# A two-layer graph network on one core: attributes' linear scores made in layer 0, codes loaded two steps ahead, a narrower placing product

## The chip, the cores and the metric

The kernel runs on one core of a Trainium2 chip. The core has a TensorE (PE, with its weight loads shown apart as PEld), a VectorE (DVE), a ScalarE (ACT), a GpSimd (POOL) and a SyncE (SP), and 16 DMA engines. The metric is the device time in microseconds of one execution; the median of three runs stands for a kernel. Three runs of the kernel before took 3234.09, 3242.03 and 3247.2 us.

## The reference, cut to what matters

There are N = 3125 nodes with 128 features, and E = 100,000 edges sorted by destination; each edge has a source, a destination, 16 attributes and one of 4 relations.

```python
# layer 0
mean = segment_sum(x[src], dst) / max(deg, 1)
h = layernorm(x + elu(mean @ W0 + b0))
# layer 1: an attention over each (node, relation)
xl = einsum('nf,rfh->nrh', h, W_l) + b_l          # 4 heads of 128: 512 columns
xr = einsum('nf,rfh->nrh', h, W_r) + b_r
z  = xl[src, type] + xr[dst, type] + edge_attr @ W_e[type, :16] + rel_emb[type] @ W_e[type, 16:]
score[e, h] = sum_c leaky_relu(z)[e, h, c] * att[type, h, c]
alpha = softmax of score over the edges of one (dst, type)
h_msg = weighted mean over relations and heads of segment_sum(alpha * xl[src, type])
# then layernorm, a feed-forward block, layernorm, and an outer residual layernorm
```

`leaky_relu(z) = 0.8 relu(z) + 0.2 z`. So a score has a part with relu, and a part that is linear in z: 0.2 times a sum over channels of z times att. The linear part of the edge's attributes is a product of the 16 attributes with a small vector for each head and relation ("v2" below). The linear part of xl is kept in four more columns of the table of xl.

## The kernel before, in words

Edges are taken in tiles of 128; 784 tiles (TT) make 196 quads of four tiles (NQ, index u) and 98 groups of eight tiles (NGR). The work is in three parts: a prologue, layer 0, and layer 1 with a short tail.

**Order.** In both layers a wrapper class `Ordered` (L637) ties each engine's instructions to the order in which the Python code issues them, so each engine runs a list written by hand; the profile therefore shows nearly all of them under one line, L647. SP issues the loads and stores, POOL the gathers.

**Prologue (L767 to L925).** It turns sources, destinations and types into layouts by edge, and writes two tables to DRAM: `seg_d` (for each edge a code of relation and place in its window) and `rm_d` (masks for the segmented scans). It makes `tm`, a bf16 tile of 128 x 3136 which says for each edge which of the four relations is its own (L859).

**Layer 0 (L927 to L1352).** A loop over steps s, one quad per step from quad 52 on (the first 52 quads are handled by counting). In a step PE sums gathered rows of x by destination (`sums0`), ACT copies the sums (`out_copy`), PE places them (`out0`), DVE adds them (`add0`). Other work hangs on given steps through `at_step`: weights in steps 3 to 11, counting in steps 3 to 41, and for each of 25 blocks of 128 nodes a chain that ends in a burst of products (`tables`, `half`) which write 512 columns of xl and xr for four relations to DRAM. Attributes come in with edges on partitions; `turned` (L1112) transposes them for four quads at once into `emt`, and `keep` stores that to the DRAM table `eat_d`, in 49 such groups spread over the steps by `turned_at` (L1087). `edge_weights` (L980) makes the vectors of the scores: `attw` for the part with relu and `vw` for the linear part. In step NS, `rows_of_sources` turns `tm` in place into a mask of 0 and -1e30 (`tng`).

**Layer 1 (L1355 to L1719).** A loop over steps s with software pipelining: `part(f, s, lag, every, n)` calls f for the quad or group that is `lag` steps behind. For a quad u:

- `load_rows` one step ahead: on SP, in this order, `er` (attributes, 256 KB, repeated for four relations, 2 buffers), `sg` (codes, 128 KB, repeated on all partitions, 3 buffers), for even u four loads of `rm` (32.1 KB each), then one, two or four windows of xr, `win` (14 buffers; one for u under 80, two under 152, four after that). `load` has POOL gather four tiles of rows of xl, 258 KB each.
- `distance` (ACT: `far` from `sg`), `onehots` (DVE: `oht` from `sg`), `masked` (DVE: `ea` from `far` and `er`).
- one step later for each of four heads: `z_of` (PE: eight or more products into one bank of PSUM) and `relu` (ACT), then `score` (PE: four products of 32 columns of weights into `row`). `score_edges` (L1497) opens the bank `row` with four products `vw` x `ea`.
- `linear` (DVE: `lx` from the mask `tng` and the four extra columns of xl), which `score_end` adds to `row` by a transpose.
- then the segmented softmax per group, and eight steps later (`LATE`) `sums`, `sums_out`, `spread` (DVE: `ohq`, a one-hot of 128 x 128), `add_sums_p` (PE: `fo`, 128 columns) and `add_sums` (DVE adds 64 of those columns to `acc1`).

Of the kernel before, what the change touches and what calls it, by code (L numbers as in the profile page):

```python
# [9 lines left out]
F32 = mybir.dt.float32  # L10
I32 = mybir.dt.int32
U16 = mybir.dt.uint16
BF16 = mybir.dt.bfloat16
AF = mybir.ActivationFunctionType
OP = mybir.AluOpType
# [5 lines left out]
P = 128  # L21
# [3 lines left out]
R = 4  # L25
H = 4
HC = H * F
# [13 lines left out]
BIG = 1.0e30  # L41
# [3 lines left out]
F32R = mybir.dt.float32r  # L45
# [645 lines left out]
def windows(ctx: ExitStack, tc: tile.TileContext, a, out, flag):  # L691
# [5 lines left out]
    rm_d = S["rm_d"] = dram.tile([TT, RW], BF16, name="rm_d")  # L697
    fl_d = dram.tile([3, TT], F32, name="fl_d")
    eat_d = dram.tile([NQ, 2 * DE, 512], F32, name="eat_d")
    xl_d = dram.tile([NP * R, XW], F32, name="xl_d")  # L700
    xr_d = dram.tile([NP * R * 2, HC], F32, name="xr_d")
    h_d = dram.tile([NB2, P, F], F32, name="fh_d")
# [9 lines left out]
    pid = cst.tile([P, 1], I32, name="pid")  # L712
    ir = cst.tile([P, R], F32, name="ir")
    attw = cst.tile([P, H, 2, WA], F32, name="attw")
    vw = cst.tile([P, 2, WA], F32, name="vw")
    tm = tng = cst.tile([P, TT, R], BF16, name="tmr")
    rv = cst.tile([P, NQ], F32, name="rv")
    weh = cst.tile([P, HC], F32R, name="weh")
    wel = cst.tile([P, HC], F32R, name="wel")
# [31 lines left out]

    with tc.tile_pool(name="l0c", bufs=1) as l0c:
        acc0 = l0c.tile([P, 2, NPW], F32, name="acc0")

        XG, TD = 24, 4 * UD
        xg = l0c.tile([P, XG, F + 1], F32, name="xg")
# [10 lines left out]
        with tc.tile_pool(name="pr", bufs=1) as pr, tc.tile_pool(name="prp", bufs=2, space=PSUM) as prp:  # L767
# [64 lines left out]
            for k, t1 in ((2, 4 * UP), (4, 4 * UQ)):  # L832
# [23 lines left out]
            nc.vector.tensor_scalar_min(dc_i, rF4[:, :UD, 0], float(ND - 1))  # L856
            typ = floats("typ", typi)
            to_e(typ_e, typ)
            nc.vector.tensor_tensor(tm, typ_e.unsqueeze(2).to_broadcast([P, TT, R]),  # L859
                                    ir.unsqueeze(1).to_broadcast([P, TT, R]), op=OP.is_equal)  # L860


            seg = pr.tile([TR, TC, P], BF16, name="seg")
# [63 lines left out]
        with tc.tile_pool(name="m0c", bufs=1) as m0c, tc.tile_pool(name="l0", bufs=2) as l0, \  # L927
# [7 lines left out]
            def at_step(s, eng, f):  # L935
                jobs.setdefault((s, eng), []).append(f)
# [24 lines left out]
            cr = l0e.tile([DR + 1, R], F32, name="cr")  # L961
            nc.vector.memset(cr, 1.0)

            def load_edge_weights():
                for i in range(2):
                    for r in range(R):
                        p0 = r * 2 * DE + i * DE
                        sp.dma_start(we[p0:p0 + DE], a["L1_gnn_W_e"][r, 0:DE, :])
                        sp.dma_start(attr[p0:p0 + DE], bcast(a["L1_gnn_att"][r], HC, DE))
                sp.dma_start(arow, a["L1_gnn_att"].rearrange("r h c -> (r h) c"))  # L970
# [9 lines left out]
            def edge_weights():  # L980
                act.activation(weh, we, AF.Copy)
                ve.tensor_sub(wel, we, weh.bitcast(F32))
                ve.tensor_mul(attr, attr, we)
                v2 = l0e.tile([P, H], F32, name="v2")
                ve.tensor_reduce(v2, attr.rearrange("p (h c) -> p h c", h=H), AX.X, OP.add)
                ve.tensor_scalar(v2, v2, SLOPE, None, op0=OP.mult)
                atp_ = bank()[:, 0, :R * H]
                pe.transpose(atp_, arow, ident[:R * H, :R * H])
                ve.memset(attw, 0.0)
                ve.memset(vw, 0.0)  # L990
                for i in range(2):
                    ve.tensor_copy(vw[:, i, 16 * i:16 * i + 16].rearrange("p (h r) -> p h r", r=R),
                                   v2.unsqueeze(2).to_broadcast([P, H, R]))
                    for h in range(H):
                        ve.tensor_scalar(attw[:, h, i, 16 * i + 4 * h:16 * i + 4 * h + 4],
                                         atp_.rearrange("p (r h) -> p h r", r=R)[:, h], 1.0 - SLOPE, None, op0=OP.mult)

            def places():

                fbv = fb.rearrange("p (u i) -> p u i", i=4)  # L1000
                i4 = l0e.tile([P, 4], F32, name="i4")
                ve.tensor_scalar(i4, iw[:, :4], p5, None, op0=OP.is_equal)
                ve.tensor_scalar(rv, fbv[:, :, 0], -1.0, p31, op0=OP.mult, op1=OP.add)
                for i in range(4):
                    ve.scalar_tensor_tensor(rv, fbv[:, :, i], i4[:, i:i + 1], rv, op0=OP.mult, op1=OP.add)

            def rows_of_sources():

                ve.tensor_scalar(tng, tm, 1.0, BIG, op0=OP.subtract, op1=OP.mult)
                ve.tensor_scalar_min(typ_e, typ_e, float(R - 1))  # L1010
                ve.scalar_tensor_tensor(src_e, src_e, R, typ_e, op0=OP.mult, op1=OP.add)

# [36 lines left out]
            for i, f in enumerate([edge_weights] +  # L1049
                                  [linear_weights(r) for r in range(R)] +  # L1050
                                  [constant(r) for r in range(R)]):
                at_step(3 + i, "ve", f)


            ees, erows = {}, {}
# [29 lines left out]
            NS = NQ - UD  # L1085

            def turned_at(f):  # L1087
                return f * (NS - 6) // (NQ // 4)

            def step_of(u):  # L1090
                return turned_at(u // 4)
# [20 lines left out]
            def turned(us):  # L1112
                mp = bank()
                for j, u in enumerate(us):
                    c, i0 = u // QC, u * 4 % TR
                    pe.transpose(mp[:, j], ees[c][:, i0:i0 + 4].rearrange("p t s d -> p (t s d)"), ident)
                em = l0.tile([P, 4, P], F32R, name="emt", bufs=3)
                act.activation(em, mp, AF.Copy)
                X["emt", us[0]] = em

            def keep(us):
                em = X.pop(("emt", us[0])).bitcast(F32)
                for j, u in enumerate(us):
                    sp.dma_start(eat_d[u].rearrange("x (t e) -> t x e", t=4), em[:, j])
# [189 lines left out]
            for s in range(last + 1):  # L1314
# [18 lines left out]
                    f()  # L1333
                if UD < u <= NQ:
                    out0(u - 1)
                counts = jobs.pop((s, "count"), [])
                for i, v in enumerate(counts):
                    count(v)
# [2 lines left out]
                    count_add(v)  # L1341
                if UD < u <= NQ and not counts:
                    add0(u - 1)
                for e in ("act", "ve"):
                    for f in jobs.pop((s, e), []):
                        f()
# [10 lines left out]
    with tc.tile_pool(name="ac", bufs=1) as ac, tc.tile_pool(name="at", bufs=2) as at, \  # L1357
# [51 lines left out]
        dc = at.tile([16, 1], F32, name="dc", bufs=3)  # L1409
        nc.vector.memset(dc, 0.0)  # L1410
        carry = {"m": mc, "d": dc}
        Q, G = {}, {}
        pe, ve, act, pool, sp = (Ordered(tc, e) for e in (nc.tensor, nc.vector, nc.scalar, nc.gpsimd, nc.sync))
        es = [slice(i * P, (i + 1) * P) for i in range(4)]
        cg = [slice(i * WA, (i + 1) * WA) for i in range(4)]
        hs = [slice(h * F, (h + 1) * F) for h in range(H)]

        def load_rows(u):
            d = Q[u] = {}
            d["er"] = at.tile([P, 512], F32, name="er", bufs=2)  # L1420
            ev = eat_d[u]
            sp.dma_start(d["er"], bass.AP(tensor=ev.tensor, offset=ev.offset,
                                          ap=[[0, R], [512, 2 * DE], [1, 512]]))
            d["sg"] = at.tile([P, 512], BF16, name="sg", bufs=3)
            sv = S["seg_d"][u * 4:u * 4 + 4, :]
            sp.dma_start(d["sg"], bass.AP(tensor=sv.tensor, offset=sv.offset, ap=[[0, P], [1, 512]]))
            if u % 2 == 0:
                g = G[u // 2] = {}
                g["rm"] = at.tile([P, RW], BF16, name="rm", bufs=5)
# [36 lines left out]
        def linear(u):  # L1466
            d, g = Q[u], G[u // 2]
            if u % 2 == 0:
                g["lx"] = at.tile([P, 4, 2, H, R], F32, name="lx")
            ve.tensor_tensor(g["lx"][:, :, u % 2],  # L1470
                             tng[:, u * 4:u * 4 + 4].unsqueeze(2).to_broadcast([P, 4, H, R]),
                             d["xl"][:, :, HC:].unsqueeze(3).to_broadcast([P, 4, H, R]), op=OP.add)

        def z_of(u, h):
            d = Q[u]
# [14 lines left out]

        def score(u, h):
            d, g = Q[u], G[u // 2]
            for i in range(4):
                pe.matmul(g["row"][cg[i], :], attw[:, h, u % 2], d["r", h][:, es[i]],
                                 start=False, stop=False, skip_group_check=True)

        def score_edges(u):  # L1497
            d, g = Q[u], G[u // 2]
            if u % 2 == 0:
                g["row"] = atp.tile([P, P], F32, name="row", bufs=2)  # L1500
            for i in range(4):
                pe.matmul(g["row"][cg[i], :], vw[:, u % 2], d["ea"].bitcast(F32)[:, es[i]],
                                 start=(u % 2 == 0), stop=False, skip_group_check=True)

        def score_end(g):
            d = G[g]
# [140 lines left out]

        def spread(u):
            d = Q[u]
            d["ohq"] = at.tile([P, P], F32, name="ohq")  # L1650
            ve.tensor_scalar(d["ohq"], iw, rv[:, u:u + 1], None, op0=OP.is_equal)

        def sums_out(u):
            d = Q[u]
# [2 lines left out]

        def add_sums_p(u):
            d = Q[u]
            d["fo"] = atp.tile([P, P], F32, name="fo")  # L1660
            pe.matmul(d["fo"], d["ags"], d["ohq"], start=True, stop=True)

        def add_sums(u):
            fo = Q.pop(u)["fo"]
            n = node(u * 4, ENG.DVE)
            ve.tensor_tensor(acc1[:, ds(n, WQ)], acc1[:, ds(n, WQ)], fo[:, :WQ], op=OP.add)

        def part(f, s, lag, every, n):
            i = s - lag
# [9 lines left out]
                z_of(u, h)  # L1679
                relu(u, h)  # L1680

        for s in range(-1, NQ + LATE + 2):
            u = s - 1
            part(load_rows, s, -1, 1, NQ)
            part(load, s, 0, 1, NQ)
            part(distance, s, 0, 1, NQ)
# [27 lines left out]
            part(add_sums, s, LATE, 1, NQ)  # L1714
            part(joined4_p, s, 7, 2, NGR)
            if 0 <= u < NQ:
                score_edges(u)
                score(u, 0)
                score(u, 1)  # L1719

# [122 lines left out]
```

## Time and profile before

| | us |
|---|---|
| median of three runs | 3242.03 |
| lowest, highest | 3234.09, 3247.2 |
| the profiled execution's own time | 3245.12 |
| its span, first to last instruction | 3243.3 |
| PE, PEld busy | 2474.8 (76%), 1828.0 (56%) |
| DVE busy | 1730.9 (53%) |
| ACT busy | 945.0 (29%) |
| POOL busy | 1340.8 (41%) |
| first and last `far` of layer 1 begin at | 1185.8 and 3075.4 |

How to read it: the page sums an engine's busy time over the whole span, while the three parts of the kernel have different limits, so views that are cut to a stretch of time matter more than these totals. Matmuls are pipelined and their ends are modelled: a busy PE is not a PE at its peak. fp32 products show two records for one instruction. A share of DMA time is a mean over 16 engines. Some matmul records are missing from the trace; waits that they ended show as "remote" or "another core or an unknown queue".

### The profile page before, as it was taken

Reading aid. Unit: us, or ns where it says so; the run is one execution under the profiler, and the core shown is the slowest. Engines: PE = TensorE matmul, PEld = TensorE weight load, DVE = VectorE, ACT = ScalarE, POOL = GpSimd, SP = SyncE. Lnnn points to the kernel's source line nnn. Section 1 sums busy time; section 2 is a strip of 40 time slices with the busy share of each in tenths; the row PEclk is TensorE's granted clock in tenths of the full one; section 3 lists DMA queues with packets and bytes.
Section 4 is the critical chain, followed back from the end, with each engine's and each line's share of the span. In section 5 each row is a group of like instructions: output and inputs, shape, how many; then the busy total and the mean of one; then the engine's idle time right before and its main releaser. Section 6 shows DMA issues by size and latency. Waiting matters only on the chain.

```text
span 3243.3 us, 67735 instructions
## 1 busy us (share of the span) xinstructions
PE 2474.8 (76%) x24804; PEld 1828.0 (56%) x24804; DVE 1730.9 (53%) x6219; ACT 945.0 (29%) x2071; POOL 1340.8 (41%) x1371
## 2 busy tenths in 40 slices
PE   1456666655566658999999999898999989988853
PEld 1233343333243436777777777777777777777732
DVE  6555332222222314676676666666666655555567
ACT  0111122322233323333333333333333323222311
POOL 5455545455355232444444444444444433333200
PEclk9976676766667778999999999999999998898966
DMA  4122344533345475777777777777777777787710
GB/s 121 53 69 91 115 139 140 176 113 118 127 133 166 147 236 145 206 208 192 208 203 206 205 209 216 212 220 214 217 213 221 219 207 205 206 216 203 191 32 21
DMA packets 280460, 546.46 MB, mean 168 GB/s; under 512 B 41066, under 2 KB 120784, under 8 KB 279321
## 3 DMA queue, kind: packets, MB, share of 16 engines
q1 hardware_dynamic: 195526, 295.42, 29.8%
q0 software_dynamic: 81152, 244.96, 27.9%
q8 instruction: 197, 3.23, 0.4%
q10 hardware_dynamic: 3440, 1.66, 0.3%
q14 instruction: 145, 1.19, 0.1%
HBM read 445.90 MB, written 95.95 MB: 167 GB/s over the span
## 4 chain that ended last, share of the span: by engine, by line
PE 40%; DMA 25%; DVE 11%; another core or an unknown queue 8%; issue 7%; ACT 4%; SPq 2%; DVEq 0%; ACTq 0%
DMA sg<-seg_d 17%; PE z L647 15%; PE xp L647 7%; PE row L647 5%; PE fo L647 4%; DMA er<-eat_d 4%; PE ag L647 2%; SPq L647 2%; PE sg L647 2%; DMA win<-xr_d 1%; PE mp L647 1%; PE dn L647 1%; DMA rm<-rm_d 1%; PE mw L647 1%
## 5 line engine op out<-in xcount | busy, mean ns | idle before, releaser
L647 POOL DMA_INDIRECT xl<-xl_d,src_e x784 | 778.2, 993 | 1193.8 <-PE ag L647 290.7
L647 POOL DMA_INDIRECT xg<-in_x_dram,src_e x576 | 561.0, 974 | 526.6 <-PE sg L647 308.5
L647 ACT ACTIVATE relu<-z 128x512 f32<-128x512 f32 x784 | 446.6, 594 | 629.4 <-PE z L647 400.5
L647 PE MATMUL z<-f_ident,xl 128*128 128x128 f32 x3136 | 501.2, 282 | 20.6 <-issue 18.7
L647 PE MATMUL z<-ea,weh 128*128 128x512 f32 x784 | 399.4, 509 | 72.2 <-ACT relu L647 44.8
L647 PEld LDWEIGHTS z<-f_ident,xl 128*128 128x128 f32 x3136 | 381.6, 145 | 72.7 <-issue 28.8
L647 PE MATMUL z<-oht,win 96*128 96x128 f32 (+2 forms) x1600 | 365.4, 309 | 39.3 <-issue 21.8
L647 PEld LDWEIGHTS z<-oht,win 128*128 128x128 f32 (+1 forms) x1600 | 292.4, 200 | 111.4 <-issue 31.1
L647 PE MATMUL fo<-ohq,sgs 128*128 128x64 f32 x576 | 137.6, 384 | 267.7 <-ACT sgs L647 164.8
L647 ACT ACTIVATE far<-sg,pm 128x512 bf16<-128x512 bf16 x196 | 141.3, 721 | 646.9 <-DMA sg<-seg_d 546.4
L647 PE MATMUL z<-ea,wel 128*128 128x512 f32 x784 | 320.5, 409 | 3.3 <-issue 3.1
L647 DVE TENSOR_SCALAR oht<-sg,p 128x512 fp32r<-128x512 bf16 x196 | 95.9, 489 | 386.6 <-DMA sg<-seg_d 330.8
L647 PEld LDWEIGHTS fo<-ohq,sgs 128*128 128x128 f32 x576 | 116.6, 284 | 319.4 <-ACT sgs L647 204.0
L647 DVE TENSOR_TENSOR acc<-acc,fo 128x64 f32 (+1 forms) x340 | 84.0, 247 | 393.6 <-PE fo L647 122.6
L647 PE MATMUL row<-relu,attw 128*32 128x128 f32 x6272 | 269.0, 286 | 12.9 <-issue 12.6
L647 PEld LDWEIGHTS z<-ea,weh 128*128 128x128 f32 x784 | 153.8, 196 | 166.0 <-issue 102.5
L647 PE MATMUL ag<-xl,wo 128*32 128x128 f32 x6272 | 219.6, 281 | 3.4 <-DVE wo L647 3.4
L647 PE MATMUL xp<-cbl,two 128*128 128x512 f32 x200 | 176.8, 884 | 41.2 <-ACT xlr L647 25.4
L647 PEld LDWEIGHTS row<-relu,attw 128*32 128x32 f32 x6272 | 176.2, 114 | 53.5 <-issue 50.4
L647 DVE TENSOR_TENSOR xh<-xp,xh 128x512 fp32r<-128x512 f32 x100 | 69.1, 691 | 223.5 <-ACT xh L647 177.9
L647 PEld LDWEIGHTS ag<-xl,wo 128*32 128x32 f32 x6272 | 165.0, 112 | 7.3 <-DVE wo L647 3.7
L647 PEld LDWEIGHTS z<-ea,wel 128*128 128x128 f32 x784 | 156.7, 200 | 4.6 <-issue 4.5
(311 smaller groups left out, 3606.8 us busy)
## 6 DMA issues: line engine op xcount, KB each, us to landing
win<-xr_d SPq DMA_DIRECT2D x224, 256.0 KB
xr_d<-xh SPq DMA_DIRECT2D x100, 512.0 KB
er<-eat_d SPq DMA_DIRECT2D x196, 256.0 KB
win<-xr_d SPq DMA_DIRECT2D x176, 192.0 KB
xl_d<-xlr SPq DMA_DIRECT2D x100, 258.0 KB
sg<-seg_d SPq DMA_DIRECT2D x196, 128.0 KB
rm<-rm_d SPq DMA_DIRECT2D x392, 32.1 KB
eat_d<-emt SPq DMA_DIRECT2D x196, 64.0 KB
```

The source lines that it names most:

```text
L647: ins = f(*args, **kw)
```

## The change

Three things change together.

1. The linear part of the attributes' scores moves from layer 1 to layer 0. For each of the 49 groups of four quads, layer 0 now multiplies the transposed attributes (`lin`: four products of 64 columns, whose stationary operand is `emt` and whose moving operand is the new `vt`), adds the mask of the relations (`lin_add`), and stores 128 x 256 values to a new DRAM table `lb_d`. Layer 1 loads these once per four quads (`LB`), and `linear` adds the four extra columns of xl to them. `score_edges`, `vw` and the mask tile in the long-lived pool go; the mask `tng` is made in the prologue. `edge_weights` moves from step 3 to step 1 (and what follows it by two steps as well); to build `vt` it sends v2 through DRAM (`v2_d`). The groups of attributes start at step 5, and `emt` has two buffers in place of three.
2. `sg` is loaded by a function of its own, `load_codes`, two steps ahead, with four buffers, and stands ahead of `load_rows` in SP's order.
3. The one-hot that places sums in layer 1, and its product `fo`, have 64 columns in place of 128.

```diff
@@ layer 0: pools and masks
-    vw = cst.tile([P, 2, WA], F32, name="vw")
-    tm = tng = cst.tile([P, TT, R], BF16, name="tmr")
+        tng = l0c.tile([P, TT, R], BF16, name="tng")
...
+            nc.vector.tensor_tensor(tng, typ_e.unsqueeze(2).to_broadcast([P, TT, R]),
                                     ir.unsqueeze(1).to_broadcast([P, TT, R]), op=OP.is_equal)
+            nc.vector.tensor_scalar(tng, tng, 1.0, BIG, op0=OP.subtract, op1=OP.mult)
@@ edge_weights
+                sp.dma_start(v2_d, v2)
+                vd = l0e.tile([P, R, H], F32, name="vd")
+                    for t in range(4):
+                        sp.dma_start(vd[32 * t:32 * t + 32], v2_d.rearrange("(r x) h -> x r h", r=R))
+                for t in range(4):
+                    ve.tensor_scalar(vt[:, t].rearrange("p h r -> p r h"), vd, i4[:, t:t + 1], None, op0=OP.mult)
-                ve.memset(vw, 0.0)
-                    ve.tensor_copy(vw[:, i, 16 * i:16 * i + 16].rearrange("p (h r) -> p h r", r=R),
-                                   v2.unsqueeze(2).to_broadcast([P, H, R]))
@@ rows_of_sources
-                ve.tensor_scalar(tng, tm, 1.0, BIG, op0=OP.subtract, op1=OP.mult)
@@ schedule
-                at_step(3 + i, "ve", f)
+                at_step(1 + i, "ve", f)
-                return f * (NS - 6) // (NQ // 4)
+                return 5 + f * (NS - 10) // (NQ // 4)
@@ groups of attributes
-                em = l0.tile([P, 4, P], F32R, name="emt", bufs=3)
+                em = l0.tile([P, 4, P], F32R, name="emt", bufs=2)
+            def lin(us):
+                em = X["emt", us[0]].bitcast(F32)
+                ln = X["ln"] = m0p.tile([P, 4, 4, H * R], F32, name="mw")
+                for j in range(4):
+                    pe.matmul(ln[:, j], em[:, j], vt, start=True, stop=True)
+            def lin_add(us):
+                lb = X["lb"] = l0.tile([P, 16, H, R], F32, name="lb")
+                ve.tensor_tensor(lb, X.pop("ln").rearrange("p j t (h r) -> p (j t) h r", r=R),
+                                 tng[:, t:t + 16].unsqueeze(2).to_broadcast([P, 16, H, R]), op=OP.add)
             def keep(us):
+                sp.dma_start(lb_d[us[0] // 4], X.pop("lb").rearrange("p t h r -> p (t h r)"))
@@ the step of layer 0: lin after out0, lin_add after add0
+                for us in edges:
+                    lin(us)
...
+                for us in edges:
+                    lin_add(us)
@@ layer 1
+        def load_codes(u):
+            d = Q[u] = {}
+            d["sg"] = at.tile([P, 512], BF16, name="sg", bufs=4)
+            sp.dma_start(d["sg"], ...)
+            if u % 4 == 0:
+                LB[u // 4] = at.tile([P, 4, 4, H, R], F32, name="lb")
+                sp.dma_start(LB[u // 4].rearrange("p j t h r -> p (j t h r)"), lb_d[u // 4])
-            d["sg"] = at.tile([P, 512], BF16, name="sg", bufs=3)
-                             tng[:, u * 4:u * 4 + 4].unsqueeze(2).to_broadcast([P, 4, H, R]),
-                             d["xl"][:, :, HC:].unsqueeze(3).to_broadcast([P, 4, H, R]), op=OP.add)
+                             LB[u // 4][:, u % 4], d["xl"][:, :, HC:].unsqueeze(3).to_broadcast([P, 4, H, R]), op=OP.add)
-        def score_edges(u):
-            for i in range(4):
-                pe.matmul(g["row"][cg[i], :], vw[:, u % 2], d["ea"].bitcast(F32)[:, es[i]],
-                                 start=(u % 2 == 0), stop=False, skip_group_check=True)
-            d["ohq"] = at.tile([P, P], F32, name="ohq")
+            d["ohq"] = at.tile([P, WQ], F32, name="ohq")
-            d["fo"] = atp.tile([P, P], F32, name="fo")
+            d["fo"] = atp.tile([P, WQ], F32, name="fo")
-        for s in range(-1, NQ + LATE + 2):
+        for s in range(-2, NQ + LATE + 2):
+            part(load_codes, s, -2, 1, NQ)
             part(load_rows, s, -1, 1, NQ)
```

## The prediction

> **What bounds the kernel now.** I read the page first, then busy time by stretches, then the waits, then the order of time inside one pair of steps, and last the packets of the DMA queues. The stretches (columns: stretch, its length, busy time and count of PE, PEld, DVE, ACT, POOL, granted clock, DMA share, GB/s):
>
> ```profile
> 450.00:1150.00 700.00, 434.93 (x1912) 257.89 (x1912) 207.49 (x680) 209.38 (x476) 323.37 (x340) 0.67 0.43 141
> 1300.00:1900.00 600.00, 567.48 (x7203) 440.64 (x7200) 412.30 (x1450) 222.67 (x476) 268.62 (x273) 0.98 0.73 205
> 1950.00:2550.00 600.00, 547.69 (x6922) 445.32 (x6910) 380.20 (x1341) 203.26 (x438) 253.32 (x253) 0.95 0.75 216
> 2620.00:3020.00 400.00, 354.20 (x4236) 294.05 (x4234) 218.17 (x765) 115.16 (x252) 143.46 (x144) 0.91 0.78 208
> ```
>
> Row 1 is layer 0, rows 2 to 4 are layer 1 with one, two and four windows a quad. Counting the writes of `ea` in the trace, these rows hold 68, 63 and 36 steps: 8.82, 9.52 and 11.11 us a step. PE looks like the bound of layer 1, but its ends are modelled, and GB/s stands near 210 while the bytes of a step grow. So I turned to waits and to one pair of steps:
>
> ```profile
> ACT far L647 <- DMA sg<-seg_d: 546.4, 116, 11.5
> DVE oht L647 <- DMA sg<-seg_d: 330.8, 75, 10.3
> ```
> ```profile
> 1607.49 0.62 SPq L647 DMA_DIRECT2D er<-eat_d  x1
> 1608.36 0.32 SPq L647 DMA_DIRECT2D sg<-seg_d  x1
> ...
> 1615.77 0.38 SPq L647 DMA_DIRECT2D sg<-seg_d  x1
> 1616.19 4.95 SPq L647 DMA_DIRECT2D rm<-rm_d  x4
> ...
> 1618.96 0.72 ACT L647 ACTIVATE far<-sg,pm 128x512 bf16<-128x512 bf16 x1 [2.39 <-DMA sg<-seg_d]
> ```
>
> The codes issued at 1608.36 are those that `far` waits for until 1618.9: 10.5 us for 128 KB. Steps alternate: the writes of `ea` lie 7.5 us apart on average after odd quads and 10.0 after even ones (stretch of row 2). Why is a small load so slow? `rm` has 32 partitions from two source rows, `er` comes from a source whose slowest dimension is 4.
>
> [...] in 1300 to 1900 us SP's queue has 40.2 four-byte semaphore packets a step, and 16 (`win`) + 16 (`sg`) + 4 (`er`) + 4 (two `rm` of two) is 40; and at 1609 us 44 `rm` packets of 49 ns begin in one us, which is two engines' worth. [...] Now the work of engines 0 and 1 in a step, with the median packet times of the trace: 16 packets of gathers (4128 B, 167 ns) 2.67, `er` 32 x 87 ns 2.78, `rm` 32 x 49 ns 1.57, `win` 8 x 87 ns 0.70, `sg` 8 x 46 ns 0.37, semaphores 0.09: 8.2 us of 8.82. With two windows 8.9 of 9.52, with four 11.2 of 11.11 (packets there take 99 to 213 ns). With mean packet times it is over 100% in all three. And in row 2 fewer than two packets are under way for 0.3% of the time only, while five or fewer are for 20% of it: gathers, `er` and `rm`, the rest that the lowest engines still have to do. So layer 1 is set by DMA engines 0 and 1; PE and the wait for `sg` follow them.
>
> Layer 0 is different. Its chain, by line, in 420 to 1130 us:
>
> ```profile
> by line: PE xp L647 25.0%; another core or an unknown queue 24.4%; PE fo L647 7.6%; issue 7.4%; SPq L647 5.7%; PE sg L647 5.4%; PE mw L647 3.8%; PE mp L647 3.1%; ACT L647 2.4%; ACT sgs L647 2.1%; ACT xlr L647 1.8%; DVE as L647 1.5%; DMA xr_
> ```
>
> The unknown waits that I opened (DVE to 706.25, ACT to 708.51) end on the semaphore that PE's `sg` and `z` products raise, so these are PE's unrecorded matmuls. PE is then 25.0 + 24.4 + 7.6 + 5.4 + 3.8 + 3.1 = 69% of the chain there, at a clock of 0.67. DMA is at 43%, gathers land within 4 us of issue and some 40 us before use.
>
> **The change part by part.** The sum is made against the profiled execution, 3245.1 us (3.1 above the median).
>
> *Products leave layer 1.* `score_edges` is eight records; at 1608.57 and 1616.15 the next line begins 0.24 us later. `fo` loses 64 of 128 columns in two records:
>
> ```profile
> L647 PE MATMUL fo<-ohq,ags 128*128 128x128 f32 x90 | 22.5, 334 | 7.4 <-DVE ea L647 2.5 <-DVE ohq L647 2.3 <-ACT relu L647 1.9
> L647 PE MATMUL row<-ea,vw 128*32 128x128 f32 x360 | 19.9, 294 | 0.0
> L647 PE MATMUL sm_p<-rsum,f 128*128 128x32 f32 x44 | 7.3, 249 | 0.0
> ```
>
> 128 against 32 columns is 85 ns, so 64 fewer are 57 ns, twice: 0.11. Together 0.35 us a step, 69 us of PE over 196 steps. I put it at nothing: behind it lie engines 0 and 1, whose packets it doesn't touch. If they weren't full it would be worth up to 69. `ohq` on DVE (0.28 us) shrinks by at most half, 27 us in all, under the same cover.
>
> *Codes two steps ahead.* No byte is removed. `sg` goes in front of `er`'s wait for `masked`, its four buffers were last read two steps before, and the 10.5 us then have two steps. The 546 us of ACT's wait go, but what is late next is `er`: in the pair shown it was issued 0.9 us before `sg` in the same queue, so it lands hardly sooner, and with engines 0 and 1 full its landing moves to where their work ends. Value: 0; if they weren't full, see the first rival.
>
> *`lb` loads.* 49 loads of 128 rows of 1 KB: eight packets each on every engine. `sg`'s packets of the same size take 46 (median) to 66 ns (mean): 18 to 26 us on engines 0 and 1. I take +22. SP's issue, 0.35 us each like `sg`, is hidden where SP waits for `ea`.
>
> *`lin` in layer 0.* 49 groups of four fp32 products with 64 moving columns, each with its own 128-column weights: the shape of `fo<-ohq,sgs`. Four such records at 699.90 occupy PE for 1.04 us, and 0.66 when the clock is up (735.31): 0.26 to 0.165 each, 0.21 in the middle. Eight records, 1.7 us a group, 82 us of PE. At 69% of the chain: +57, between 20 (mostly in PE's gaps) and 90. `lin` stands between `out0` and `sums0`, so a quad's sums, ACT's `sgs` and the gathers that reuse its buffers queue behind it. It needs `emt`, whose copy (0.60) ACT starts after `sgs` (0.28); `out0` takes that long too, so I see no added wait. [...]
>
> *`lin_add`.* DVE, 256 columns from PSUM; `A<-A,dn` takes 363 ns for 200 and 468 for 300: 0.42, 21 us, and DVE is off the chain: +1. But `mean`, the next user of the one `mw` bank, waits for it: about 0.65 us in a third of 25 blocks, +4.
>
> *`edge_weights` at step 1.* DVE stands behind a store of v2, four loads that wait for it, and their landing. A small load took 2 to 3.7 us in this stretch (`xf`, 104 to 152 us), so two trips are some 6 us; DVE is on the path there (busy 66% of the first 100 us). +6, from 0 to 8. The mask's second operation, 0.97 us, moves from step NS to the prologue: 0 to +1, I take 0.
>
> *Stores of `lb_d`*, 0.5 us of SP and eight packets an engine per group, under a DMA share of 43%: 0; without that cover 25. `emt` with two buffers: a group comes about every third step of 7.3 us, so its stores have some 20 us per group: 0.
>
> Sum: 3245.1 + 22 + 57 + 1 + 4 + 6 = 3335; against the median 3332.
>
> **The rivals.** *The wait was the bound, not the engines' throughput (not slower).* For: `ea` after odd quads comes every 7.5 us, PE then being the limit, and by median times engines 0 and 1 have 7% to spare in the first two thirds. Then steps fall to 8.2 + 0.1, 8.9 + 0.1 and stay at 11.1: 80 x 0.5 + 72 x 0.5 = about 80 us gained, less 68 in layer 0 (57 + 1 + 4 + 6): about 3230. It decides where engines 0 and 1 need under 8.2 us a step. Against: hardly a moment without two packets. *`lin` hides in PE's gaps* (it is idle 265 of 700 us by record): layer 0 costs some 10 in all, about 3275 with `lb`. *SP's queue:* each load waits for the one eight before it to land (SP waits 66.7 us for `er` in 2620 to 3020 us), so 49 more loads take a place each: 10 us of landing by 8 is 1.25, 61 us in place of the 22: 3371. Against: where engines are full, the queue's length changes nothing.
>
> **How the numbers follow.** Forecast 0.58, at 3332, with its own range 3290 to 3385; not slower 0.20, around 3230; hidden `lin` 0.14, around 3275; the queue 0.08, 3371 and above. Measurement tells 0.5%, 16 us: faster is below 3226, half of the first rival, 0.11; within is its other half and the lowest of hidden `lin`, 0.12; slower 0.77. The range 3225 to 3390 leaves out 0.1 below and under 0.1 above.
>
> **What would show it.** Right: no `row<-ea,vw`, `far` no longer waiting for `sg`, `ea` waiting for `er` instead; steps of row 2 still 8.8 to 9.0 us; PE's busy share in layer 1 lower, DMA's equal; the first `ea` some 65 us later than 1186.6. Wrong: steps of 8.3 us or less in row 2, or a first `ea` within 25 us of the old one.

## The result and the profile after

The changed kernel takes 3261.88 us (median of 14 runs, 3242.1 to 3269.96), the kernel before 3243.81 in the same comparison (14 runs, 3224.12 to 3254.38): a ratio of 1.0062, 95% interval 1.0038 to 1.0085. It is slower by 18 us by the medians and by 20 by the ratio, where 3332 was forecast: the direction and the range held, the size did not (90 us were forecast over the median of before). The first write of `ea`, which marks the end of layer 0, comes at 1234.8 us, 48 later than before, where some 65 were forecast. The profiled execution of after took 3242.1 us, the lowest of its 14 runs, so the two profiles together would even show a small gain; where the time went is read by stretches, and its amount from medians.

Busy time by stretches, kernel after, the same four stretches and columns as before:

```profile
450.00:1150.00 700.00, 462.80 (x2116) 295.48 (x2116) 200.19 (x632) 194.49 (x439) 333.73 (x352) 0.66 0.42 139
1300.00:1900.00 600.00, 567.78 (x6898) 436.32 (x6897) 431.17 (x1514) 231.89 (x501) 269.33 (x274) 0.99 0.72 212
1950.00:2550.00 600.00, 547.41 (x6530) 441.79 (x6528) 391.60 (x1381) 210.22 (x453) 259.29 (x260) 0.94 0.74 224
2620.00:3020.00 400.00, 353.78 (x4084) 293.29 (x4082) 229.70 (x803) 123.31 (x264) 149.29 (x151) 0.90 0.78 218
```

In layer 0 PE is busy for 28 us more of 700 (434.93 before), and has 204 more records. In layer 1 PE is busy just as long as before, with 305 and 392 records fewer in the two stretches of 600 us, and more steps fit: the writes of `ea` in rows 2 to 4 number 72, 65 and 37 in place of 68, 63 and 36, which is 8.33, 9.23 and 10.81 us a step in place of 8.82, 9.52 and 11.11. A count in a window can be off by a step. Over the same quads (the first 80, the next 72 and the last 43) a step takes 8.73, 9.30 and 10.93 us in place of 9.06, 9.53 and 11.18.

The longest wait on ACT in 1300 to 1900 us, kernel after, and then the wait that headed `far`'s list there before (columns: total, times, longest):

```profile
ACT relu L647 <- PE z L647: 314.0, 191, 3.9
```
```profile
ACT far L647 <- DMA sg<-seg_d: 127.7, 35, 7.4
```

`far` no longer appears among the long waits. ACT waits for PE instead (`relu` on `z` was 146.4 us before), and what PE waits for is seen in the chain. The chain of the same stretch, by line, first of after and then of before:

```profile
by line: PE z L647 29.5%; DMA er<-eat_d 19.8%; DMA win<-xr_d 9.4%; PE row L647 8.1%; PE ag L647 4.5%; DMA rm<-rm_d 4.4%; issue 4.1%; SPq L647 4.0%; DVE ea L647 2.3%; DVE wo L647 1.9%; PE fo L647 1.9%; DVE de L647 1.8%; PE sm_p L647 1.3%; DV
```
```profile
by line: PE z L647 26.0%; DMA sg<-seg_d 25.5%; DMA er<-eat_d 10.4%; PE row L647 9.2%; issue 5.6%; PE ag L647 4.2%; DVE ea L647 2.7%; PE fo L647 2.5%; DVE f L647 2.1%; DVE m L647 1.4%; DVE y L647 1.3%; DVE de L647 1.3%; PE sm_p L647 1.0%; DV
```

The codes' 25.5% are gone. The attributes (`er`) took over nine points of them, the windows of xr (9.4%) and `rm` (4.4%) most of the rest. SP's queue and ACT's `far`, kernel after, show the new order (start, length, what):

```profile
1606.21 0.72 ACT L647 ACTIVATE far<-sg,pm 128x512 bf16<-128x512 bf16 x1 [0.20 <-DVE ea L647]
1606.99 0.38 SPq L647 DMA_DIRECT2D sg<-seg_d  x1
1607.47 1.13 SPq L647 DMA_DIRECT2D lb<-lb_d  x1
1610.52 0.63 SPq L647 DMA_DIRECT2D er<-eat_d  x1
...
1614.67 0.71 ACT L647 ACTIVATE far<-sg,pm 128x512 bf16<-128x512 bf16 x1
```

`far` starts without a wait for codes. In layer 0 the new work has these rows (450 to 1150 us, groups by form):

```profile
L647 PE MATMUL mw<-vt,emt 128*128 128x64 f32 x256 | 53.3, 376 | 21.1 <-issue 14.0 <-ACT emt L647 6.6
L647 PEld LDWEIGHTS mw<-vt,emt 128*128 128x128 f32 x256 | 48.2, 281 | 24.4 <-issue 16.1 <-ACT emt L647 7.4
L647 DVE TENSOR_TENSOR lb<-mw,tng 128x256 f32<-128x256 f32 x32 | 13.6, 424 | 48.1 <-PE mw L647 17.8 <-remote 16.1 <-PE sg L647 11.6
```

`mw<-vt,emt` is `lin`: 53.3 us by 256 records is 0.208 us, where 0.21 was estimated, and `lin_add` takes 0.424 where 0.42 was. Over all of layer 0 `lin` has 84.9 us of records, 82 by the estimate. So the prices of the operations were right; what they cost on the path is another matter.

### The profile page after: what moved, and what is told of

It is laid out like the page before. It is cut to its first block, busy times and chain, and to the rows that moved or that the text cites. A ratio compares the mean times of both kernels' runs of the same rounds, so it can differ in the third digit from the quotient of the medians.

```text
span 3240.2 us, 65657 instructions
## 1 busy us (share of the span) xinstructions
PE 2504.2 (77%) x23628; PEld 1855.7 (57%) x23628; DVE 1745.0 (54%) x6269; ACT 945.9 (29%) x2071; POOL 1339.4 (41%) x1371
## 4 chain that ended last, share of the span: by engine, by line
PE 27%; DMA 21%; DVE 7%; issue 3%; SPq 2%; POOL 1%; ACT 0%; DVEq 0%; POOLq 0%; ACTq 0%
PE z L647 17%; DMA win<-xr_d 11%; DMA er<-eat_d 8%; PE row L647 4%; PE ag L647 3%; SPq L647 1%; PE fo L647 1%; PE sm_p L647 1%; POOL xl L647 1%; DVE ea L647 1%; DMA rm<-rm_d 1%; DVE wo L647 1%; DVE f L647 1%; DVE de L647 1%; SPq L734 0%
## 5 line engine op out<-in xcount | busy, mean ns | idle before, releaser
L647 ACT ACTIVATE relu<-z 128x512 f32<-128x512 f32 x784 | 455.9, 597 | 1211.9 <-PE z L647 922.7
L647 PE MATMUL z<-oht,win 96*128 96x128 f32 (+2 forms) x1600 | 383.8, 317 | 137.4 <-DMA win<-xr_d 90.9
L647 DVE TENSOR_TENSOR_SCAN m<-rm,row 128x128 f32<-128x128 bf16 x98 | 41.3, 421 | 395.0 <-PE row L647 395.0
L647 PE MATMUL ag<-xl,wo 128*32 128x128 f32 x6272 | 226.7, 287 | 3.2 <-DVE wo L647 3.2
L647 PEld LDWEIGHTS row<-relu,attw 128*32 128x32 f32 x6272 | 154.2, 112 | 53.0 <-issue 41.6
L647 DVE SCALAR_TENSOR_TENSOR ea<-far,er 128x512 fp32r<-128x512 bf16 x196 | 134.0, 684 | 68.0 <-issue 35.8
```

The costliest lines, as they stand in the source:

```text
L647: ins = f(*args, **kw)
```

## The experiments

The expectations set theories against each other. In the two profiles layer 1 is 53 us shorter with the change (1838.2 in place of 1891.7), which the prediction did not have. **A**: the few DMA engines that carry `er` and `rm` set layer 1, and the 53 us come from the codes' early load, because a queue that is never empty lets these engines do a little more. **B**: they come from PE's products that left. **C**, in the later runs: these engines have room, and what counts is when a load that is waited for lands.

Which engines a load runs on (0 and 1, 0 to 3), and how many packets that puts on each, is my estimate wherever the prediction and the expectations say it: no trace names the engine of a packet. What the trace of before shows in 1300 to 1900 us is that a load of `rm` has at most three records of its landing and one of `er` at most five, where `sg` and `win` have up to 16 (`lb` too, in the trace of after); and that the third last record of an `sg` load comes 5.0 us after its issue and the last one 9.9 (medians of 66 loads).

Changes are given as differences of ratios to the kernel before; the "first `ea`" (end of layer 0) and the length of layer 1 (first to last `ea`) are counted in each run's trace. One profile scatters: before and the run with the codes alone have the same code ahead of layer 1, and the first `ea` at 1186.6 and 1208.2. So amounts come from medians, and profiles say where.

**The codes alone.** The kernel before with the second part of the change only (three buffers).

```diff
+        def load_codes(u):
+            d = Q[u] = {}
+            d["sg"] = at.tile([P, 512], BF16, name="sg", bufs=3)
+            ...
-        for s in range(-1, NQ + LATE + 2):
+        for s in range(-2, NQ + LATE + 2):
+            part(load_codes, s, -2, 1, NQ)
```

> The kernel before with only the codes' load moved two steps ahead of its use and in front of load_rows (three buffers, since a fourth doesn't fit beside the old mask). Theory A (DMA engines 0 to 3 set layer 1, and a queue that is never empty there lets them do a little more; layer 1's gain of 53 us between the first and the last write of ea comes from this part): layer 1 some 50 us shorter than before, 1840 us, and the whole 3190 to 3200. Theory B (the gain comes from PE's products that left): same as before within 10 us.

Measured: 3224.52 us beside 3245.27, ratio 0.9936 (0.992 to 0.9953). This part alone gains 21 us: less than the 45 to 55 of A, more than B allows, and the prediction had put it at nothing.

**The codes put back.** The changed kernel with `sg` loaded in its old place; the first and third part stay.

```diff
-            d["sg"] = at.tile([P, 512], BF16, name="sg", bufs=4)   # in load_codes
...
+            d["sg"] = at.tile([P, 512], BF16, name="sg", bufs=3)   # in load_rows, after er
```

> The changed kernel with the codes' load put back to its old place (one step ahead, behind er, three buffers): the linear scores from layer 0 and the narrow product stay. Theory A: layer 1 loses all of its gain and pays for lb, 1890 to 1915 us between the first and last ea, whole 3300 to 3320. Theory B: layer 1 keeps its gain, whole about 3260.

Measured: 3277.87, ratio 1.012 (1.0086 to 1.0153), 39 us over before and so 19 over the changed kernel. The whole lies between what A and B gave. The codes are worth about 20 us in either surrounding.

**The products of `vw` taken out, nothing in their place.** `score_edges` goes from the kernel before, and the first `score` opens the bank.

```diff
-                score_edges(u)
+            first = u % 2 == 0 and h == 0
+            if first:
+                g["row"] = atp.tile([P, P], F32, name="row", bufs=2)
-                                  start=False, stop=False, skip_group_check=True)
+                                  start=first, stop=False, skip_group_check=True)
```

> The kernel before without score_edges: the attributes' linear part of the scores is left out of the computation, so this is PE's saving alone (0.24 us a step, 47 us over 196), with no work added in layer 0 and no lb. Theory A: within 10 us of before, since PE waits for the DMA engines. Theory B: 40 to 55 us faster than before.

Measured: 3241.57, ratio 0.9991 (0.9975 to 1.0007). Alone, what these products take from PE in layer 1 is worth nothing that these runs can tell, as forecast. The narrower `fo`, 22 us of records by the prediction's prices, was not tried apart.

**No `lin`.** The changed kernel without its four products a group; `lin_add` copies the mask in place of adding it.

```diff
-                for us in edges:
-                    lin(us)
-                ve.tensor_tensor(lb, X.pop("ln").rearrange(...), tng[...], op=OP.add)
+                ve.tensor_copy(lb, tng[...])
```

> The changed kernel without the four products of lin in each group; lb is then the mask alone (the attributes' linear part is left out), with its stores, loads and order as they are. My sum put lin at 57 us of layer 0 (82 us of PE at 69%): 55 us faster than the changed kernel, first ea about 1180. If the extra 48 us of layer 0 come from elsewhere (v2's trip through DRAM, stores of lb, two buffers of emt), it is under 15 us faster.

Measured: 3222.11, ratio 0.9919 (0.989 to 0.9947). Against the changed kernel's 1.0062 `lin` costs 1.43%, 46 us; 57 were forecast. The first `ea` comes at 1217.1, not at the 1180 expected, and only 18 us before that of the changed kernel; but this profile is the slowest run of its six and the changed kernel's the fastest of its 14, so the amount is taken from the ratios.

**Are two source rows dear?** The changed kernel with one more load of 128 KB for every second quad, which nothing reads: once from two source rows, and once from sixteen.

```diff
+            if u % 2 == 0:
+                g["xx"] = at.tile([P, 512], BF16, name="xx", bufs=2)
+                sp.dma_start(g["xx"], bass.AP(..., ap=[[RW, 2], [0, P // 2], [1, 512]]))    # extra_on_2
+                sp.dma_start(g["xx"], bass.AP(..., ap=[[RW, 16], [0, P // 16], [1, 512]]))  # extra_on_16
```

> The changed kernel with one more load per two quads, which nothing reads: 128 rows of 1 KB from two source rows[...]. Theory A (engines 0 and 1 are all but full in layer 1): nearly all of it is paid, 98 x 3.1 = 300 us, between 200 and 300 us slower than the changed kernel. Theory C (they have room; what counts is when a waited-for load lands): the load is read by no one and most of it hides, under 100 us slower.

> The same bytes in the same place of SP's order, from sixteen source rows[...]. Theory A: 98 x 0.4 = 40 us slower than the changed kernel at most. Theory C: 0 to 15 us. The difference between this and the run with two engines is the price of the two engines alone: same bytes, same number of loads in flight.

Here the kernel before took 2959.49 us (2949.19 to 2967.72); that it is 280 us below the first comparison comes from the time up to the end of layer 0, as shown further down, so ratios are compared. Measured: 1.0973 (1.0929 to 1.1017) from two source rows, 1.0314 (1.0278 to 1.0349) from sixteen. The 3.1 and 0.4 us a pair of the expectations are an estimate: 128 packets of 49 ns, the median of `rm`'s in the trace of before, divided by two and by sixteen. The same bytes cost 196 us more from two source rows: 2.0 us for a pair of steps, where the estimate has a difference of 2.7. Layer 1 is 2072.4 us against 1879.7. Against the changed kernel's 1.0133 in a later comparison (below) the loads cost 249 and 54 us. The first is inside what A gave and far above C's 100; the second is above the 40 of A and the 15 of C. Busy time in 1100 to 1700 us, from two source rows and then from sixteen:

```profile
1100.00:1700.00 600.00, 517.75 (x5976) 397.60 (x5975) 373.19 (x1313) 203.93 (x432) 245.78 (x247) 0.91 0.66 193
```
```profile
1100.00:1700.00 600.00, 549.50 (x6620) 422.01 (x6620) 410.97 (x1444) 225.38 (x476) 266.22 (x271) 0.97 0.72 213
```

With the same bytes from two source rows, the mean DMA share is 0.66 in place of 0.72, GB/s 193 in place of 213, and PE does a tenth less (5976 records in place of 6620). I read this as two engines that hold up the rest; a mean over engines, which falls here, can't show it. SP's queue, a rival in the prediction, is not the reason: both runs have the same number of loads, and in this stretch SP waits 60 us for landings in the run with two source rows and 180 in the one with sixteen.

**The two uneven loads spread.** The changed kernel with `er`'s partitions ordered by attribute first, so that the slowest dimension of the source is 32; and, apart from it, with `rm` as one load from eight source rows in place of four from two. What reads or writes these rows (the weights and `pm`; the stores of `rm_d`) follows the new order and is left out here.

```diff
-                                          ap=[[0, R], [512, 2 * DE], [1, 512]]))
+                                          ap=[[512, 2 * DE], [0, R], [1, 512]]))       # er16
-                for i in range(4):
-                    sp.dma_start(g["rm"][i * 32:(i + 1) * 32], bass.AP(..., ap=[[4 * RW, 2], [0, 16], [1, RW]]))
+                sp.dma_start(g["rm"], bass.AP(..., ap=[[RW, 8], [0, 16], [1, RW]]))    # rm8
```

> The changed kernel with the attributes' rows laid out as (attribute, relation) in place of (relation, attribute) on partitions[...]. Same bytes, same result. Theory A: engines 0 and 1 lose 24 x 87 ns = 2.1 us of some 8.2 a step; PE's 7.2 to 8.5 us become the bound, layer 1 drops by 150 to 280 us, whole 2990 to 3110. Theory C: er lands sooner, and layer 1 drops by what it waits for er, 8 to 20% of the chain: as much. If neither holds, under 30 us.

> The changed kernel with the masks' rows stored in the order (tile mod 4, half), so that one load per two quads replaces four and has eight source rows[...]; three loads fewer on SP per pair. Theory A: engines 0 and 1 lose 48 x 49 ns = 2.35 us a pair, 1.2 us a step; engines 2 and 3 take over at some 7 us plus a little: layer 1 drops by 100 to 200 us. Theory C: under 60 us, since far and ea don't read rm.

Measured: 0.9286 (0.9251 to 0.9322) for `er`, 0.9661 (0.9623 to 0.9699) for `rm`. No byte is removed, and layer 1 falls from 1829.4 us (the changed kernel's next profile, below) to 1589.2 and 1687.6, by 240 and 142. A gave 150 to 280 and 100 to 200; C gave as much for `er`, but under 60 for `rm`. So, with the two extra loads above, the order in which these two loads take their source rows is what sets layer 1. That it does so through the number of engines is my estimate, as are the packets taken off each engine in the expectations. (`rm` as one load also spares SP three issues a pair; that was not tried apart.)

**Both spread, with and without the change, and the changed kernel beside them.** `lb_loaded_once` tests the price of the `lb` loads: the changed kernel loads the table for the first four quads and never again.

```diff
-            if u % 4 == 0:
-                LB[u // 4] = at.tile([P, 4, 4, H, R], F32, name="lb")
+            if u == 0:
+                LB[0] = ac.tile([P, 4, 4, H, R], F32, name="lb")
...
-                             LB[u // 4][:, u % 4], ...
+                             LB[0][:, u % 4], ...
```

> The changed kernel as it is, once more, so that it stands beside the other three runs under the same conditions. Its ratio to the kernel before was 1.0062. If the price of lin in layer 0 depends on how many gaps PE has there, then where layer 0 is short (about 1006 us to the first ea, as in the four runs with added or re-laid loads) it may differ from where it is long (1235): between 0.995 and 1.010.

> The changed kernel with the table of linear scores loaded once, for the first four quads, and never again: 48 loads of 128 KB leave layer 1, and all later quads use the first values, so their scores are not those of the reference. If engines 0 and 1 set layer 1, 384 packets of 1 KB leave each of them: 18 to 26 us less than the changed kernel, 0.5 to 0.8%. If these loads found room elsewhere, as the sum over the first four runs suggests, under 8 us less (0.25%).

> The changed kernel with both loads re-laid[...]. If only the lowest engines set layer 1, the two gains (212 and 101 us of the kernel before) can't add in full, because after er is spread PE is busy all the time in the stretches with one and two windows: a ratio to the kernel before of 0.92 to 0.93, like er16 alone (0.9286). If DMA engines still set a part of it, the gains add further: 0.90.

> The kernel before with the same two loads re-laid, and none of the three parts of the change. PE is then the bound of layer 1, so PE's records count there: the 0.35 us a step that the change takes off PE in layer 1 (69 us in all) should now be worth something, and lin (82 us of PE in layer 0) costs about what it did. By that the changed kernel with re-laid loads is not slower than this one: this run 0 to 1% above the changed kernel with both loads re-laid, a ratio to the kernel before of 0.92 to 0.94. If the products that leave PE are worth nothing here either, this run is 1 to 1.5% faster than that one.

Measured beside 2970.91 us of before (2955.33 to 2976.9): the changed kernel 1.0133 (1.0106 to 1.0159), outside the 0.995 to 1.010 expected; `lb` loaded once 1.0114 (1.0084 to 1.0144); both loads spread in the changed kernel 0.9165 (0.914 to 0.919), in the kernel before 0.9041 (0.9016 to 0.9066).

The `lb` loads cost some 6 us (12 either way), within what these runs can tell from nothing, in place of 22. And the last two runs went against my expectation: with the loads spread, the kernel before stays the faster one, by 37 us. Busy time of that run in layer 1 (1000 to 1600, 1700 to 2200 and 2250 to 2500 us):

```profile
1000.00:1600.00 600.00, 599.98 (x7876) 474.20 (x7873) 452.78 (x1600) 247.16 (x523) 300.91 (x300) 1.00 0.77 226
1700.00:2200.00 500.00, 499.85 (x6782) 418.63 (x6783) 374.56 (x1317) 203.40 (x431) 248.36 (x248) 1.00 0.87 257
2250.00:2500.00 250.00, 246.98 (x3329) 212.06 (x3329) 172.50 (x603) 93.06 (x199) 111.54 (x113) 1.00 1.01 264
```

PE has no gap left in the first two, and a GB/s of 226 to 264 passes where 203 to 224 did before. The chain of the first stretch is PE's alone:

```profile
by line: PE z L647 61.5%; PE row L647 18.6%; PE ag L647 11.8%; PE fo L647 5.2%; PE sm_p L647 2.9%; issue 0.0%
```

Here the change does shorten layer 1: it is 1556.7 us with the change and 1591.7 without, 35 us of the 69 by record. I put that down to the products that leave PE; they were not tried apart here. But the end of layer 0 lies at 1009.6 with it and 928.1 without, 81 us for `lin` and the small terms of layer 0. That didn't fit 46 us and 11, and led to the last four runs.

**The sum once more, where layer 0 is short.** The kernel before itself, the changed kernel without `lin`, the codes alone, and the codes alone on top of the spread loads.

```diff
         def load_codes(u):
+            d["sg"] = at.tile([P, 512], BF16, name="sg", bufs=3)      # codes_with_relaid_loads: on er16 and rm8 of before
```

> The kernel before itself, for its trace under the same conditions as the next three. If lin's price is what PE's idle time lets through, layer 0 ends here at some 930 us (the kernel before with re-laid loads: 928.1), some 80 us before the changed kernel's 1009.8, with PE busy for a larger share of layer 0 than the 62% in the first profile. If the changed kernel's layer 0 differs by only 46 us again, it ends at some 965. Ratio 1.000.

> The changed kernel without the four products lin of each group, so the table of linear scores holds whatever the bank held plus the mask. If lin costs its whole PE time where layer 0 is short: 1.0133 less 0.027 (82 us), 0.986. If it costs 46 us as before: 0.998.

> The kernel before with the codes loaded two steps ahead and nothing else. It was 0.9936 of the kernel before. Layer 1 has the same length under both conditions, so the same 20 us: 0.993.

> The kernel before with [...]one load of rm in place of four, and the codes two steps ahead. With the loads re-laid the kernel before shows no wait for sg among the longest, and PE busy 100% of the stretches with one and two windows. If the codes' 20 us came from engines 0 and 1 being full, nothing of it is left: 0.902 to 0.906, like the kernel before with both loads re-laid (0.9041). If the wait itself was worth it: 0.897.

Measured beside 2961.66 us (2948.07 to 2968.0): the kernel before 0.999 (0.9976 to 1.0004); no `lin` 0.9915 (0.9889 to 0.994); codes alone 0.9918 (0.989 to 0.9945); codes with spread loads 0.9098 (0.9073 to 0.9122), which is not below the 0.9041 without them but above it, and above both values expected. So the 20 us of the codes exist only as long as the loads are uneven. (In the runs without `lin` the table holds the mask alone, as the first edit shows, and not what the bank held.) By stretches (450 to 900 us), the kernel before here:

```profile
450.00:900.00 450.00, 360.17 (x1627) 214.90 (x1627) 165.69 (x570) 181.36 (x412) 273.20 (x287) 0.74 0.56 188
```

and the changed kernel here:

```profile
450.00:900.00 450.00, 375.95 (x1752) 243.03 (x1751) 156.97 (x514) 166.84 (x374) 289.85 (x305) 0.70 0.57 185
```

PE is busy by record for 80% of this stretch of layer 0, against 62% (434.93 of 700) in the first profile. `lin` costs 1.0133 − 0.9915 = 2.2%, 65 us here and 46 there; 0.9915 lies between the two values expected. The place between two profiles says the same: no `lin` ends layer 0 at 941.2, the changed kernel at 1009.8, before at 924.8. Up to that point PE is idle by record for 275 us without `lin` and for 257 with it. So 18 of `lin`'s 85 us went into PE's gaps, and 67 came on top.

The whole, from ratios (us against before):

| | layer 0 long (before 3244) | layer 0 short (before 2966) |
|---|---|---|
| changed kernel | +20 | +39 |
| `lin` | +46 | +65 |
| codes ahead, alone | −21 | −24 |
| the rest | −5 | −2 |

The changed kernel and the codes carry 5 to 8 us of uncertainty, `lin`, a difference of two comparisons, some 12, the rest more.

## Why the prediction was wrong in size, point by point

**Right.** Layer 1 is bound by how `er` and `rm` are loaded: with `er` alone spread the changed kernel is at 0.9286 of before, where it is at 1.0133 in another comparison as it stands, and the same bytes from two source rows cost 196 us more than from sixteen. That a few engines are what these loads fill was my estimate; the runs agree with it, and none shows which engines. The products of `vw` that leave PE in layer 1 are worth nothing by themselves (0.9991), and `er` is what became late next (19.8% of the chain in place of 10.4%). The small terms of layer 0 (`lin_add` 1, `mean` 4, the trip of v2 6) made 11 us, and their sum fits: without `lin`, the changed kernel ends layer 0 at 941.2 us against 924.8 to 931.9 for the two profiles with the old layer 0 beside it, 9 to 16 us.

**Wrong, first: the step "Codes two steps ahead … Value: 0".** It is 21 to 24 us. I took engines 0 and 1 for full, with an estimated 8.2 us of work in 8.82 (by median packet times of the trace of before), and the 7% between as error of the packet times. Some of it was room: row 2 went to 8.33 us a step, near the 8.2 + 0.1 of the first rival, and over the same 80 quads the step fell by 0.33 us of the rival's 0.5. Rows 3 and 4 went to 9.23 and 10.81 where it said 9.0 and 11.1; 10.81 is under the 11.2 us that I had estimated for these engines there, so that estimate was too high. My evidence against the rival, that hardly a moment has fewer than two packets under way, can't tell: that is still so after the change (0.2% of the time in row 2), because the count runs over all engines. So "a few engines set the pace" and "the wait is worth time" were no alternatives. The account that fits both is that a late `sg` kept these engines from their next work for part of each pair. The link may be `er`'s two buffers, freed by `masked`, which waits for `far` and so for `sg`. What SP waited for `ea` before it could issue a load (1300 to 1900 us) fits this, in the kernel before, with the codes alone and in the kernel after:

```profile
SPq L647 <- DVE ea L647: 72.6, 25, 5.3
```
```profile
SPq L647 <- DVE ea L647: 7.9, 7, 2.8
```
```profile
SPq L647 <- DVE ea L647: 6.1, 3, 3.0
```

More buffers for `er` were not tried, so the link is not shown. That the value of the codes is gone once the loads are spread is.

**Wrong, second: "`lb` loads … I take +22".** The run that loads the table once gives 6 us (0.2%, not told from 0). Room on the few engines would explain it, but that is not shown: the extra load from sixteen source rows has the same 128 KB as a load of `lb`, and 98 of it cost some 54 us, 0.6 us each, where 48 loads of `lb` cost some 0.1 each.

**Mis-sized: "`lin` … 69% of the chain: +57".** 82 us of records was right. The share that counts was 46 / 82 = 56% in one comparison and 65 / 82 = 79% in the other, with some 14 points of uncertainty each. 57 lies between, so this term is not what failed.

**A reading that was wrong.** The prediction took waits on an unknown source in layer 0 for PE's unrecorded matmuls. No matmul records are missing: the two profiles of the kernel before, the two with the codes ahead and the two with its loads spread have 24,804 each, and the changed kernel has exactly the 1568 of `score_edges` fewer and the 392 of `lin` more. In the first profile 127 waits of DVE, ACT and POOL in layer 0 are put down to "remote". All end on PE's semaphore, 1.5 to 16 us after the recorded end of the last product that raises it. In `before_2` there is none. So, as far as these records go, PE's products finish later in the first profile than their records end, and its 62% there doesn't tell how far PE was held up.

**The other rivals.** `lin` did not hide in PE's gaps (46 and 65 us of 82). SP's queue would have made the `lb` loads cost 61 us; they cost some 6. The first rival, that the wait was the bound, had the right part and too much of it: about 80 us, where the codes gained 21 to 24.

**Open.** After `lin` and the codes, a rest of −5 to −2 us includes the trip of v2 and the like (some +11) and the `lb` loads (some +6), so about 20 us more were gained somewhere. Layer 1 is shorter in a profile of the changed kernel (1829.4) than with the codes alone (1850.1), by that amount: PE's 69 us may be worth some 20 once the codes no longer wait, as the change was worth 35 with the loads spread. Two profiles of the kernel before differ by more (1891.7 and 1864.7). The uncertainties of the ratios are as large as this, so it is not shown.

Against the sum: layer 0 was forecast at +68 and layer 1 at +22. By ratios and the traces layer 0 cost 57 (46 + 11) to 76 (65 + 11), and layer 1 gained some 37 in both: the half of the sum that failed is layer 1, where the codes were put at nothing and `lb` at 22.

## What to carry to other kernels

Where a load repeats a few source rows over all partitions, try another order of its rows: the records of its landing may be few (here at most three for `rm` and five for `er`, up to 16 for other loads), and a mean DMA share of 0.73 to 0.78 hid the bound here. Re-ordering the partitions of one load was worth over eight points (1.0133 to 0.9286), where the whole change cost 1.3. Engines that an estimate finds 93% full (8.2 of 8.82 us) may still have room, and an earlier landing is then worth something: here 21 to 24 us, about a quarter of what the rival gave it, where the sum had nothing. Work put on an engine in a stretch where it is not the bound all the time costs what does not go into its gaps: here 46 and 65 us of 82.

The version that beats both kernels is the kernel before with `er` and `rm` spread: 2686.07 us, 0.9041 of before.

## What was not expected of the hardware

The kernel before took 3244 and 3245 us in two comparisons and 2959 to 2971 in three others. Its layer 1 is nearly the same in both (1891.7 and 1864.7 us in the two profiles); the first `ea` comes at 1186.6 and 924.8. In the long form DVE, ACT and PE show waits in layer 0 that the profile puts down to "remote" or to nothing (DVE `acc` 72 us and ACT `sgs` 123 us to "remote" in 250 to 900 us, neither among the long waits of the short form). As said above, they end on PE's semaphore, late after PE's records. The records themselves are hardly longer: PE's `sg` products take 388 ns on average in the long form and 375 in the short, and up to the first `ea` PE is busy by record for 696 and 668 us, idle for 490 and 257. What holds PE up was not settled. Each comparison ran on one chip: the second on chip 3, those with the short form on chips 13, 11 and 1, and for the first the record names none. So the form may go with the chip; no chip is known to have shown both, and this is not shown either. For a change that puts work into layer 0 it matters: this one costs 0.6% in the one form and 1.3% in the other.
